# Layer 0's last steps become a stream of the written order, and the first state-space prologue moves into the two-pass steps

## The chip, the cores and the metric

The kernel runs on one NeuronCore of a Trainium2 chip. The metric is the device time in microseconds. The kernel before took 868.06 us (median of three runs, 865.57 to 869.98). The engines are called PE (matrix), DVE (vector), ACT (scalar), POOL (GpSimd) and SP (synchronisation, which here issues most transfers). Each has its own instruction queue and works it off in order.

## The reference, cut to what matters

Two batches of 256 tokens with 256 features pass two layers. All arithmetic is in 32-bit floats.

```
x = x + cross_attention(layernorm(x), ctx)       # layer 0: 16 heads of 16, 4096 context rows of 128
x = x + state_space(layernorm(x))                # conv of 4, silu, 16 states scanned over the tokens, gate, layernorm
x = x + real(ifft(fft(layernorm(x)) @ w)) + bias # spectral layer
x = x + softmax((q Wq + bq)(ctx Wk + bk)^T) (ctx Wv + bv)   # layer 1: one head, 4096 context rows
x = x + self_attention(layernorm(x))             # 16 heads, only the 5 queries with the greatest score per head are kept
x = x + mixture_of_experts(layernorm(x))         # 8 experts of 256 x 1024, 2 per token
```

The state-space layer is `h = h * A + u * b`, `y = sum over states of h * c + D * u`, for 16 states of each feature. The spectral layer is linear, so the kernel forms one 256 x 256 matrix from the transform and the weights and multiplies by it.

## The kernel before, in words

**Layer 0.** The 16 heads are taken in 4 groups of 4 heads, for 2 batches: 8 groups, `G`. Each group has 16 steps in each of two passes. The first pass computes scores with the queries in rows and only takes their maxima (`mp`, DVE). The second pass, 17 steps later, computes them with the keys in rows, with the negated maxima folded into the queries (`lowered`), exponentiates them (`exps`, ACT), multiplies by the values (`weigh`, into `av`) and adds the result up on DVE. So steps 0 to 16 do the first pass alone, steps 17 to 127 do both (the two-pass steps), and steps 128 to 145 do the second pass alone: these are the last steps. `finished` divides a group by its sums and writes its part of `O[b]`. The PSUM banks are two double tiles (`ps2`) and four single ones (`ps1`, `bank`). Small work such as new keys and values is hung onto step numbers in the table `made` and is issued at the end of its step.

**State-space layer.** `state_prologue(b)` adds layer 0's output (`add_rows`), normalises, transposes (`turned`), computes the gate, the convolution of four taps and the two silus, and the projections `bcT`. For batch 0 it avoids ACT's other function tables: the root is taken by Newton steps on DVE (`rstd_by_vector`), and silu is an exponential, an addition, a reciprocal and a product. For batch 0 it runs in the last steps, one piece for each of steps 128 to 145 (`ahead`, lines 1079 to 1081). `state_loop(b)` takes 16 states one after another: `weighted` scales by b (ACT), `into` transposes (PE), `scan` scans (DVE), `outof` transposes back and scales by c, one row tile on DVE and one on ACT, and `summed` adds ACT's one up in PSUM by a product with the identity. `state_epilogue`, `spectral_layer`, `context_scores`, `context_sums`, `self_attention` and `router` follow for each batch.

**The written order.** After the last steps, two generators hold the two batches' chains: `a` is batch 1 from its prologue on, `b` is batch 0 from its state loop on. A third, `m`, forms the spectral matrix. The string `ORDER` (line 32) says letter by letter which generator runs to its next `yield`; `in_order` makes every engine keep the order in which instructions are then issued. Each batch has four PSUM banks of its own there, and `m` shares those of batch 0. Batch 1's chain can start only when the last steps have finished `O[1]`, and its states use the room that held layer 0's `exps`.

**Shared rooms.** SBUF is reused by tag: the states of batch 0 lie where values were (`V0`), the spectral inputs where keys were (`K0`), the rows of the context (`nat`) where queries (`Q`) and then the spectral inputs were. The router's result starts the experts: twelve blocks of 128 tokens always, with weights loaded into rooms that the attention gave up.

The file records nearly every instruction through one helper, so most profile rows say L164; they are told apart by their tiles.

Of the kernel before, what the change touches and what calls it, by code (L numbers as in the profile page):

```python
# [12 lines left out]
ALU = mybir.AluOpType  # L13
# [15 lines left out]
LOWEST = -3.0e38  # L29

# [3 lines left out]
        "mbbbabbambamaabmbaabmaabaaababmbbabmababaaabaamambbbbbbaabaaaaaaaaaaaaaaaaaaabaa",  # L34
        "bbaabbabbababababbabaaaaababbbbaaaaababababbaaabbabaaabaabbabbaaaaaaaaaabbbbbbba",
        "abaabbbbbbabbabaabbabbbaabaaaaaaabababaabababaabbabbbbbbabbabbbbbaaababbbbaababb",
        "bbbababaabbabaababaababababbaabababbababaaaaabbabbaaababbbabaaabababbbaabbb",
# [5 lines left out]
def perceiver(ctx: ExitStack, tc: tile.TileContext, d: dict, out: bass.AP):  # L43
# [128 lines left out]
    def rstd_of(mv):  # L172

        n = mv.shape[1]
        r = small.tile([P, n], F32, tag="rstd", name="rstd")
        ve.tensor_scalar_add(r, mv[:, :, 1], EPS)
        ve.reciprocal(r, r)
        se.activation(r, r, AF.Sqrt)
        yield 1.0
        return r  # L180

    def rstd_by_vector(mv):
# [8 lines left out]
        yield 0.5  # L191
# [4 lines left out]
        yield 2.4  # L196
        return r

    def normalised(src, dst, rstd_of=rstd_of):
# [7 lines left out]
        yield 1.2  # L207
# [5 lines left out]
        yield 0.8  # L213

    def turned(src, dst, ps):

        for c in range(2):
            for t in range(2):
                te.transpose(
                    ps[:, c * NQ + t * P : c * NQ + (t + 1) * P], src[:, t, c * P : (c + 1) * P], ident  # L220
                )
        se.copy(dst.rearrange("p c n -> p (c n)"), ps)

# [25 lines left out]
    def lower(q, negm, ps):  # L249

        for qt in range(2):
            te.transpose(
                ps[:, qt * P : (qt + 1) * P], negm[:, qt, :, :].rearrange("p j r -> p (j r)"), ident
            )
        ve.tensor_tensor(q, q, ps[:, :NQ], ALU.add)

    def add_rows(b, src, w, bank):

        srcT = XNT(b)
        turned(src, srcT, bank("ps_tr"))  # L260
        yield 1.2
# [3 lines left out]
        yield 1.6  # L265
        ve.tensor_tensor(of(b), of(b), ps.rearrange("p (t e) -> p t e", t=2), ALU.add)
        yield 0.8
# [43 lines left out]
    def spectral_matrix(bank):  # L311


        def product(terms, dst, scale):

            ps = bank("ps_f")
            for i in range(2):
# [6 lines left out]
                yield 1.8  # L324
            se.mul(dst.rearrange("p i n -> p (i n)"), ps, scale)
            yield 0.6

        se.mul(sp["ncos"], sp["cos"], -1.0)
        yield from product([(sp["wr"], sp["cos"]), (sp["wi"], sp["sin"])], sp["reT"], 1.0)
        yield from product([(sp["wr"], sp["sin"]), (sp["wi"], sp["ncos"])], sp["nimT"], 1.0)  # L330
        yield from product([(sp["reT"], sp["cos"]), (sp["nimT"], sp["sin"])], spectral, 1.0 / D)

    def state_prologue(b, bank):
# [5 lines left out]
        turned(xn, xnT, bank("ps_tr"))  # L339
        yield 1.2  # L340
        yield 0.0
# [14 lines left out]
        for i in range(2):  # L356
            project(pg[:, i * NQ : (i + 1) * NQ], gate_w, slice(i * P, (i + 1) * P), xnT)

        for c in range(2):
            se.mul(u[:, c, :], xnT[:, c, :], cols[:, c, CONV_W + 3 : CONV_W + 4])  # L360
        yield 1.0
        for c in range(2):
# [5 lines left out]
            yield 1.3  # L368
        if b == 0:
# [5 lines left out]
            for i, (col, z, o) in enumerate(  # L375
# [4 lines left out]
                yield 1.0  # L380
                ve.tensor_scalar_add(e, e, 1.0)
                ve.reciprocal(e, e)
                for c in range(2):
                    ve.scalar_tensor_tensor(o[:, c, :], z[:, c, :], cols[:, c, col : col + 1], e[:, c, :], ALU.add, ALU.mult)
                yield 2.0
        else:
            for c in range(2):
                se.activation(u[:, c, :], u[:, c, :], AF.Silu, bias=cols[:, c, CONV_B : CONV_B + 1])
            for i in range(2):
# [3 lines left out]
            yield 1.6  # L393

        ps = bank("ps_ut")
        for t in range(2):
            for c in range(2):
                te.transpose(ps[:, t * D + c * P : t * D + (c + 1) * P], u[:, c, t * P : (t + 1) * P], ident)
        pb = bank("ps_bct")
        for t in range(2):  # L400
            project_rows(pb[:, t * 2 * NS : (t + 1) * 2 * NS], u, t, bcw)
        yield 1.2
        se.copy(ut.rearrange("p t e -> p (t e)"), ps)
        ve.tensor_tensor(
# [3 lines left out]
        yield 1.0  # L408
        U[b] = dict(u=u, ut=ut, yT=yT, ub=ub, h=h, gT=gT, hc=hc, bcT=bcT, xn=xn)

    def state_loop(b, bank, by_vector):
# [28 lines left out]
        def outof(n):  # L440

            ps = bank("ps_ht")
            for t in range(2):
                for c in range(2):
                    te.transpose(
                        ps[:, t * D + c * P : t * D + (c + 1) * P], a["h"][n % 3][:, c, t * P : (t + 1) * P], ident
                    )
            for t in range(2):
# [12 lines left out]
        weighted(0)  # L461
        into(0)
        weighted(1)
        yield 1.0
        for n in range(NS):
            scan(n)
            if n + 1 < NS:
                into(n + 1)
            if n + 2 < NS:
                weighted(n + 2)  # L470
            yield 0.9
            if n >= 1:
                outof(n - 1)
            if n >= 2:
                summed(n - 2)
            yield 0.9
        outof(NS - 1)
        summed(NS - 2)
        yield 1.0
        summed(NS - 1)  # L480
        if by_vector < 2:
            se.copy(yT[:, 1, :], yps[:, :D])
        yield 0.8

    def state_epilogue(b, bank):
        a = U[b]
        ve.tensor_tensor(of(b), of(b), rows[:, LN_B, :].unsqueeze(1).to_broadcast([P, 2, D]), ALU.add)
        y = a["ub"][0]
# [6 lines left out]
        yield 0.8  # L495
        for c in range(2):
# [3 lines left out]
            )  # L500
        ve.tensor_mul(y, y, a["gT"])
        yield 1.7

# [3 lines left out]
        zs = [ps[:, t * D : (t + 1) * D] for t in range(2)]  # L507
        for t in range(2):
            te.matmul(zs[t], lhsT=ident, rhs=a["xn"][:, t, :], start=True, stop=False)
            te.matmul(zs[t], lhsT=ident, rhs=rows[:, OUT_B, :], start=False, stop=False)  # L510
            for c in range(2):
                te.matmul(
                    zs[t], lhsT=y[:, c, t * P : (t + 1) * P], rhs=out_w[:, c, :], start=False, stop=(c == 1)
                )
        yield 2.0
        for t in range(2):
            ve.bn_stats(st[:, t, :], zs[t])
            ve.bn_aggr(mv[:, t, :], st[:, t, :])
        yield 1.3
# [9 lines left out]
        yield 1.8  # L529


    def spectral_layer(b, bank):
# [3 lines left out]
        turned(xn, xnT, bank("ps_tr"))  # L536
        yield 1.2
        ps = bank("ps_s")
        for t in range(2):
            o = ps[:, t * D : (t + 1) * D]  # L540
            te.matmul(o, lhsT=ident, rhs=rows[:, FFN_B, :], start=True, stop=False)
            for c in range(2):
                te.matmul(
                    o, lhsT=xnT[:, c, t * P : (t + 1) * P], rhs=spectral[:, c, :], start=False, stop=(c == 1)
                )
        yield 1.4
        ve.tensor_tensor(of(b), of(b), ps.rearrange("p (t e) -> p t e", t=2), ALU.add)
        yield 0.8
# [8 lines left out]
    def context_scores(b, bank):  # L557
# [3 lines left out]
        turned(xn, xnT, bank("ps_tr"))  # L561
        yield 1.2
        qT = acts.tile([P, 2, NQ], F32, tag=f"O{b}", name="qT")
        ps = bank("ps_q1")
        for i in range(2):
# [1005 lines left out]
```

## Time and profile before

| what | value |
|---|---|
| median of three runs | 868.06 us (865.57 to 869.98) |
| the profiled execution | 865.26 us |
| its span | 863.5 us |
| mean granted clock of PE | 0.973 |
| busy PE, PEld, DVE, ACT | 814.6, 586.5, 571.9, 458.8 us |
| last two-pass step ends | about 445.1 us |
| the last steps, to their last `av` addition | 445.1 to 497.7 us |
| experts begin | about 749.5 us |

PE's records include the latency of a product and overlap; its busy share therefore says less than that of DVE or ACT. [...]

### The profile page before, as it was taken

How to read it: one execution, taken by the hardware profiler on the slowest of the kernel's cores; microseconds unless marked ns; L12 is line 12 of the kernel's file. 1: busy time of each engine (PE TensorE's matmuls, PEld its weight loads, DVE VectorE, ACT ScalarE, POOL GpSimd, SP SyncE). 2: the span in 40 equal slices, each digit the busy share in tenths (PEclk: the TensorE clock that was granted, in tenths of full speed). 3: DMA queues.
4: the chain of work that ended last, by engine and by line, in shares of the span. 5: the costliest groups of instructions: out<-in, count | busy, mean ns of one | idle time of the engine just before them, and what ended most of it. 6: DMA issues, size and time to landing. Idle time of an engine off the chain costs nothing.

```text
span 863.5 us, 20999 instructions
## 1 busy us (share of the span) xinstructions
PE 814.6 (94%) x8640; PEld 586.5 (68%) x8640; DVE 571.9 (66%) x1044; ACT 458.8 (53%) x858; POOL 46.1 (5%) x108
## 2 busy tenths in 40 slices
PE   5999999999999999999999899878999999699996
PEld 3665666666666666666665478756488866499995
DVE  4788888878787878788863668985743376641112
ACT  6436666766666666666668758621642225411120
POOL 5004020000000000000000000000000000030003
PEclk9999999999999999999999989998999969889999
DMA  7216131011010010000010203000222500529602
GB/s 269 55 32 184 24 115 42 21 23 23 17 23 20 19 23 19 22 19 2 2 51 2 80 19 86 13 1 1 97 98 98 195 1 2 195 70 329 229 20 81
DMA packets 35314, 56.67 MB, mean 66 GB/s; under 512 B 5872, under 2 KB 22816, under 8 KB 35216
## 3 DMA queue, kind: packets, MB, share of 16 engines
q1 hardware_dynamic: 27904, 41.44, 15.8%
q0 software_dynamic: 3264, 10.05, 3.6%
q10 hardware_dynamic: 4048, 3.80, 1.5%
q8 instruction: 70, 1.15, 0.6%
q14 instruction: 28, 0.23, 0.1%
HBM read 42.16 MB, written 4.85 MB: 54 GB/s over the span
## 4 chain that ended last, share of the span: by engine, by line
PE 83%; DVE 8%; ACT 4%; issue 2%; DMA 1%; POOL 1%; ACTq 0%; POOLq 0%; DVEq 0%
PE ps L164 29%; PE av L164 17%; PE ps_h L1362 5%; PE ps_y L1378 4%; PE ps_s L164 4%; DVE states L164 4%; PE ps_k L164 4%; PE ps_v L164 3%; PE ps_aqk L164 2%; PE ps_am L164 2%; PE ps_pt L164 1%; PE ps_ht L164 1%; PE asc L164 1%; PE ps_q L164 1%; PE ps_f L164 1%
## 5 line engine op out<-in xcount | busy, mean ns | idle before, releaser
L164 DVE TENSOR_REDUCE mp<-ps 128x2 f32<-128x1024 f32 (+1 forms) x273 | 302.6, 1153 | 88.4 <-PE ps L164 88.4
L164 ACT ACTIVATE exps<-ps 128x512 f32<-128x512 f32 (+1 forms) x495 | 263.8, 617 | 111.4 <-PE ps L164 111.1
L164 PE MATMUL ps<-qk,KB 32*128 32x256 f32 x2048 | 250.0, 392 | 1.7 <-DVE qk L164 1.7
L164 PE MATMUL ps<-KB,qk 32*128 32x256 f32 x2048 | 244.8, 390 | 0.0
L164 PEld LDWEIGHTS ps<-KB,qk 32*128 32x128 f32 x2048 | 172.1, 184 | 52.6 <-issue 37.7
L164 PEld LDWEIGHTS ps<-qk,KB 32*128 32x128 f32 x2048 | 183.9, 184 | 13.2 <-issue 4.8
L164 PE MATMUL av<-exps,V 128*32 128x256 f32 x2048 | 137.9, 387 | 2.7 <-DVE more L164 1.6
L164 PEld LDWEIGHTS av<-exps,V 128*32 128x32 f32 x2048 | 53.9, 109 | 66.4 <-ACT exps L164 37.9
L164 DVE TENSOR_TENSOR av<-av 128x256 f32<-128x256 f32 x120 | 49.4, 412 | 20.4 <-PE av L164 20.4
L1369 ACT ACTIVATE room<-ps_h 128x512 f32<-128x512 f32 x24 | 14.2, 597 | 72.5 <-PE ps_h L1362 60.3
L1362 PEld LDWEIGHTS ps_h<-room,w 128*128 128x128 f32 x384 | 44.5, 192 | 0.5
L1362 PE MATMUL ps_h<-room,w 128*128 128x128 f32 x384 | 44.8, 275 | 0.0
L164 DVE TENSOR_TENSOR_SCAN states<-decay,ps_in 128x256 f32<-128x256 f32 x64 | 39.7, 667 | 5.4 <-PE ps_in L164 5.4
L1378 PE MATMUL ps_y<-w,room 128*128 128x256 f32 x192 | 43.3, 379 | 0.0
L164 PEld LDWEIGHTS ps_v<-l_wv,ctxT 128*128 128x128 f32 x256 | 32.6, 191 | 15.4 <-issue 6.3
L1378 PEld LDWEIGHTS ps_y<-w,room 128*128 128x128 f32 x192 | 35.6, 190 | 4.4
L164 PE MATMUL ps_v<-l_wv,ctxT 128*128 128x128 f32 x256 | 35.0, 280 | 1.2 <-ACT V L164 1.2
L164 PE MATMUL ps_k<-ctxT,wkc 128*128 128x512 f32 x64 | 35.5, 640 | 0.0
L164 PE MATMUL av<-more,nat 128*128 128x256 f32 x128 | 32.9, 381 | 0.3 <-ACT more L164 0.3
L164 ACT COPY qk<-ps_k 128x512 f32<-128x512 f32 x32 | 18.6, 587 | 25.5 <-PE ps_k L164 25.5
L164 ACT ACTIVATE states<-states,more 128x256 f32<-128x256 f32 x64 | 28.2, 498 | 6.6 <-PE ps_in L164 5.9
L164 ACT ACTIVATE aexps<-asc 128x512 f32<-128x512 f32 x32 | 17.0, 604 | 24.7 <-PE asc L164 24.7
(302 smaller groups left out, 901.1 us busy)
## 6 DMA issues: line engine op xcount, KB each, us to landing
w<-in_moe_w SPq DMA_DIRECT2D x24, 1024.0 KB, 7.7
KB<-qk SPq DMA_DIRECT2D x220, 32.0 KB, 2.0
ctxT<-in_ctxT SPq DMA_DIRECT2D x4, 512.0 KB, 8.0
ctxT<-in_ctxT POOLq DMA_DIRECT2D x4, 512.0 KB, 6.3
x_slots<-O POOLq DMA_DIRECT2D x15, 128.0 KB, 6.4
y_slots<-room ACTq DMA_DIRECT2D x10, 128.0 KB, 3.5
room<-x_slots ACTq DMA_DIRECT2D x9, 128.0 KB, 5.0
KB<-qk ACTq DMA_DIRECT2D x32, 32.0 KB, 2.0
```

Source lines behind the costliest of these rows:

```text
L164: i = getattr(self.engine, name)(*args, **kw)
L1362: nc.tensor.matmul(ps[fc // 4][:, (fc % 4) * P : (fc % 4 + 1) * P], lhsT=weights[k][0][:, c, fc * P : (fc + 1) * P], rhs=xT[k][:, c, :], s ...
L1369: nc.scalar.activation(hT[k][:, 4 * i : 4 * i + 4, :].rearrange("p f n -> p (f n)"), ps[i], AF.Silu)
L1378: nc.tensor.matmul(ps[:, :D], lhsT=hT[k][:, fc, :], rhs=weights[k][1][:, fc, :], start=(fc == 0), stop=(fc == NF - 1),)
```

## The change

1. **The last steps become a stream.** A step of layer 0 is now a generator, `attend(n)`. Steps 0 to 127 are run to their end as before. Steps 128 to 145 form a fourth stream `t`, and the written order interleaves it with `b` and `m`. In these steps the exps come in four single banks, where there were two single ones and a double one.
2. **One ring of eight banks.** All streams take their PSUM banks from one pool of eight; the four for each batch are gone.
3. **Finer steps.** Almost every instruction group has a `yield` of its own, so the written order has 879 letters where it had 315. In self-attention the exponentials and maxima now come ahead of the lowering of the next group.
4. **The first prologue** runs in steps 95 to 125: one item in each of steps 95 to 111, then two items a step from 114 to 122, one in 123 and 124, three in 125. Its gate product is copied to SBUF at once, and its reciprocals come in halves of 256 columns.
5. **Fewer products.** Batch 0's state loop takes both row tiles on DVE (`by_vector` 2), so its sums in PSUM are gone. Biases and the residual are added on DVE where identity products did it. The two projections of layer 1's queries and keys are multiplied into one small matrix beforehand (`context_maps`), so that `context_scores` needs one product from `xnT` and no `qT`.
6. The load of batch 0's context rows comes after its spectral layer, where it came after its state loop.

```diff
-        ahead = state_prologue(0, bank)
-        for n in range(NM, NM + LAG + 1):
-            made.setdefault(n, []).append((next, ahead, None))
+    AHEAD = [NM - 16 - NORM + i for i in range(NORM)] + [
+        NM - 14 + i for i, k in enumerate((2, 2, 2, 2, 2, 2, 2, 2, 2, 1, 1, 3)) for _ in range(k)
+    ]
+    ahead = state_prologue(0, lambda name: bank(name))
+    for n in AHEAD:
+        made.setdefault(n, []).append((next, ahead, None))
...
-                four = [(2, False), (0, True)]
+            four = [(2, False), (0, n < NM)]
...
-        for n in range(NM + LAG + 1):
+    for n in range(NM):
+        for _ in attend(n):
+            pass
...
-    post = ctx.enter_context(tc.tile_pool(name="post", bufs=4, space=bass.MemoryType.PSUM))
-    side = [lambda name, b=b: post.tile([P, 512], F32, tag=f"s{b}", name=name) for b in range(B)]
+    post = ctx.enter_context(tc.tile_pool(name="post", bufs=8, space=bass.MemoryType.PSUM))
+    def bank(name):
+        return post.tile([P, 512], F32, tag="s", name=name)
+    def last_steps():
+        for n in range(NM, NM + LAG + 1):
+            yield from attend(n)
+        yield from finished(behind.pop("closing"))
...
-            state_loop(0, side[0], 1), later((context_rows, 0)), state_epilogue(0, side[0]),
+            state_loop(0, bank, 2), state_epilogue(0, bank), spectral_layer(0, bank),
+            later((context_rows, 0)), context_scores(0, bank), context_sums(0, bank),
...
+        "t": last_steps,
...
+        if b == 0:
+            se.copy(gT.rearrange("p c n -> p (c n)"), pg)
+            pg = gT.rearrange("p c n -> p (c n)")
...
-                ve.tensor_scalar_add(e, e, 1.0)
-                ve.reciprocal(e, e)
+                for c in range(2):
+                    ve.tensor_scalar_add(e[:, c, :], e[:, c, :], 1.0)
+                    ve.reciprocal(e[:, c, :], e[:, c, :])
...
-            te.matmul(zs[t], lhsT=ident, rhs=a["xn"][:, t, :], start=True, stop=False)
-            te.matmul(zs[t], lhsT=ident, rhs=rows[:, OUT_B, :], start=False, stop=False)
+            project_rows(ps[:, t * D : (t + 1) * D], y, t, out_w)
+            ve.tensor_tensor(zs[t], zs[t], ps[:, t * D : (t + 1) * D], ALU.add)
...
-            project(ps[:, i * NQ : (i + 1) * NQ], x1_wq, slice(i * P, (i + 1) * P), xnT)
+            te.matmul(ps[:, :NQ], lhsT=qk_w[:, c, :], rhs=xnT[:, c, :], start=(c == 0), stop=(c == 1))
```

The new function that `m` calls first:

```
def context_maps(bank):
    ps = bank("ps_wqT")
    for e in range(2):
        for c in range(2):
            te.transpose(
                ps[:, e * D + c * P : e * D + (c + 1) * P], x1_wq[:, c, e * P : (e + 1) * P], ident
            )
    yield
    se.copy(x1_wq.rearrange("p e d -> p (e d)"), ps)
    yield
    ps = bank("ps_maps")
    col = lambda e, c: cols[:, e, c : c + 1]
    for i in range(2):
        for e in range(2):
            te.matmul(
                ps[:, i * CD : (i + 1) * CD], lhsT=x1_wq[:, e, i * P : (i + 1) * P], rhs=x1_wkT[:, e, :],
                start=(e == 0), stop=(e == 1),
            )
        yield
    lhs = [lambda e: x1_wkT[:, e, :]] + [lambda e, i=i: x1_wq[:, e, i * P : (i + 1) * P] for i in range(2)]
    lhs.append(lambda e: col(e, X1_BQ).to_broadcast([P, P]))
    for k, of_e in enumerate(lhs):
        for e in range(2):
            te.matmul(
                ps[:, 2 * CD + k : 2 * CD + k + 1], lhsT=of_e(e), rhs=col(e, X1_BK if k else X1_BQ),
                start=(e == 0), stop=(e == 1),
            )
        yield
    se.copy(qk_w.rearrange("p c n -> p (c n)"), ps[:, : 2 * CD])
    se.copy(qk_b, ps[:, 2 * CD : 2 * CD + 4])
    yield
```

## The prediction

> **What bounds the kernel now.** First the page's first two parts, for shares over time; then busy time by stretch, cut where a stage begins in the order of instructions; then the groups of instructions, for the duration of one; then the list of waits.
>
> ```profile
> PE 814.6 (94%) x8640; PEld 586.5 (68%) x8640; DVE 571.9 (66%) x1044; ACT 458.8 (53%) x858; POOL 46.1 (5%) x108
> ```
>
> PE 94% is no headroom to divide by: a matmul's record is latency, not pitch. Where nothing is late (640 to 652 us) four transposes start 0.43 us ahead of what follows, two 256-column products 0.87. So I cost PE by pitch: transpose 0.108, product of 128, 256, 512 columns 0.223, 0.433, 0.86 us, one of eight quadrant-packed products 0.128.
>
> ```profile
> 397.40:445.10 47.70, 47.66 (x754) 31.91 (x755) 42.56 (x50) 32.48 (x64) 0.00 (x0) 1.00 0.01 2
> 445.10:497.00 51.90, 47.01 (x604) 27.44 (x600) 25.75 (x63) 40.30 (x68) 0.00 (x0) 0.96 0.20 57
> 497.00:525.00 28.00, 26.20 (x151) 22.19 (x147) 18.60 (x42) 17.78 (x40) 0.00 (x0) 0.90 0.04 10
> 525.00:569.00 44.00, 39.69 (x267) 32.51 (x266) 41.52 (x78) 29.83 (x72) 0.00 (x0) 1.00 0.17 49
> 569.00:592.00 23.00, 16.65 (x65) 12.80 (x64) 15.25 (x50) 4.43 (x10) 0.00 (x0) 0.85 0.00 0
> 592.00:671.00 79.00, 78.75 (x376) 57.40 (x376) 42.67 (x124) 33.03 (x57) 1.35 (x6) 1.00 0.24 80
> 671.00:749.50 78.50, 72.18 (x561) 52.48 (x559) 50.99 (x148) 30.47 (x55) 0.00 (x0) 0.91 0.31 105
> 749.50:863.50 114.00, 101.40 (x677) 95.25 (x677) 27.91 (x103) 18.91 (x33) 15.53 (x16) 0.93 0.43 140
> ```
>
> Columns: stretch, length, busy PE, PEld, DVE, ACT, POOL, granted clock, DMA share, GB/s. Row by row: the last 16 two-pass steps (2.98 us each; PE the bound, DVE idle 47.70 - 42.56 = 5.1 us, 0.32 a step); the one-pass last steps with the first prologue; the second prologue beside the first state loop; both loops (DVE 94%); epilogues and spectral layers, where no engine passes 73%; layer 1's context attention (PE); self-attention and router; the experts. From 445.1 to 749.5 are 304.4 us.
>
> ```profile
> L164 ACT ACTIVATE exps<-ps 128x512 f32<-128x512 f32 x42 | 22.6, 598 | 8.2 <-PE ps L164 7.9
> L164 DVE RECIPROCAL states<-states 128x512 f32<-128x512 f32 x2 | 6.7, 3352 | 0.1
> L164 DVE TENSOR_TENSOR_SCAN states<-decay,ps_in 128x256 f32<-128x256 f32 x64 | 39.7, 667 | 5.4 <-PE ps_in L164 5.4
> L164 ACT ACTIVATE states<-states,more 128x256 f32<-128x256 f32 x62 | 27.4, 498 | 5.9 <-PE ps_in L164 5.9
> DVE arest L164 <- PE ps_negm L164: 7.4, 7, 1.8
> ```
>
> The mean durations are the prices below; the last row, from the waits of 671 to 749.5 us, is DVE standing at the lowering of self-attention.
>
> **The change: the first prologue moves into the two-pass steps.** Seventeen items go one to a step into steps 95 to 111, 23 more into steps 114 to 125. Each stands in DVE's queue between one step's `av` addition and the next step's maxima. DVE's maxima free the two double banks of the scores, and PE waits for those.
> Steps 95 to 111: DVE gets an addition (0.68), statistics 1.2, the root by vector 2.4, two scalings 0.74: 5.0 us, against 11.2 us of DVE idle in the 16 steps 345 to 397.4 us; hidden. PE gets 8 transposes and 4 products: 2.6 us, on the path.
> Steps 116 to 122: six convolution products (2.9 us), four additions and four reciprocals of 256 columns, four products of 0.48, two tiny ones. A reciprocal of 512 columns is 3.35 us and one of 2 columns 0.17, so 256 columns are about 1.76. Splitting pays the fixed part again: by these rows 0.16 us for each of two extra reciprocals and two extra additions, 0.64 us. [...] In all 13.0 us of DVE work in seven steps that leave 7 x 0.32 = 2.2: +10.8 us on the path[...].
> Steps 114, 115, 123 to 125: the gate product, `ps_ut` and `ps_bct`: 3.1 us of PE, on the path.
> Banks: the prologue's tiles come from the ring of four single banks. `ps_tr` twice, `ps_wo` two steps, `ps_g`, `ps_ut` two, `ps_bct` together eat eight bank-steps. With three banks left, the second half's scores wait for an exp of the first half: in the step that begins at 439.1 us PE needs the bank 1.0 us into it, and the first exp ends 1.8 us into it. Between 0 (DVE already late) and 0.9 us each, 0 to 7 us; I take 4.5, nearer the upper end because none of the eight falls in the steps where DVE is late anyway.
> Sum: the last two-pass step ends 2.6 + 10.8 + 3.1 + 4.5 = **21 us later**, at 466 us (bounds 13.5 to 26).
>
> **The last 17 steps beside batch 0's state loop.** Exps: 68 of 512 columns at 0.598 = 40.7 (pairs of 1024 at 1.034 go: +0.16 x 17 = 2.8, included), 32 weightings at 0.498 = 15.9, copies 1.2: ACT 57.5 us. PE: 272 packed products 34.8, 128 transposes 13.8, context maps and the rest 6.5: 55. DVE: 32 scans 21.3, 32 weighted sums at 0.48 = 15.4 (all by vector now, so 16 ACT scalings and 16 PE sums of 0.433 go), 17 additions 7.1, rest 4: 48. ACT decides; DVE held 94% in the loops of before, so 57.5/0.92: **63 us** (58 to 74; 74 is the 78% that ACT had in the last steps of before). What waits: each `av` addition stands ahead of scans on DVE, and each `ps_in` behind scores on PE. The 2 MB `nat` load of batch 0 now stands on SP behind nothing but the spectral loads, and comes after the spectral layer; two score passes (27 us or more) cover it. Without that cover it costs the some 10 us it took at 194 GB/s.
>
> **The second prologue and first epilogue.** Batch 1 can start only when the last steps are over. Its chain: last division 0.6, transposes and copy 1.8 (the `ncos` scaling is ahead on ACT), product with the spectral one between 2.6, addition and statistics 2.0, root with table load 1.9, scaling 0.75, transposes and copy 1.3, multiplication 1.0, convolution 2.9, table load and silu 2.3, transposes 0.7, gate silu and copies 2.2, table load and weighting 2.5, `ps_in` 0.6, hand-overs 2: **25 us** (20 to 30). Batch 0's epilogue and the spectral matrix lie beside it. Full-clock PE work is only 17.6 us here. The row: 498 to 502 us, granted clock 0.50 at 3.2 of 4 us busy; the like stretch 569 to 592 had 0.85 in the mean, which costs 17.6 x 0.15 = 2.6 us. [...] I keep the row, within the hand-overs, as most of the loss is off the chain.
>
> **Batch 1's state loop with batch 0's spectral layer and scores.** DVE: 32 scans 21.3, 16 sums 7.6, 16 score copies at 0.676 = 10.8, norms and additions 6.6: 46.3; at the 94% of before **49 us**. PE has 40, ACT 32.
>
> **Both context sums and batch 1's scores.** PE: 32 x (4 x 0.108 + 2 x 0.433) = 41.6, 16 scores 13.8, epilogue, spectral and key maps 4.6: 60; before held PE full in such a stage: **62 us** (60 to 68).
>
> **Self-attention and router.** PE 57 and DVE 43 us in both kernels. The maxima now come ahead of the lowering, so part of the 7.4 us wait goes: 2.5 of it, **76 us** (70 to 80).
>
> **Fewer products.** 16 PE sums 6.9, bias and residual products of the epilogues 3.5, of the spectral layers 1.7, query products 3.5, less 3.3 for the context maps: 12 us of PE, already in the sums. They pay only where PE binds. The three DVE bias additions for each batch (0.68) are in the DVE sums.
>
> **Sum.** 63 + 25 + 49 + 62 + 76 = 275 against 304.4: -29.4; with the 21 us, **-8.4 us**. The 114 us of experts and the 865.26 - 863.5 = 1.8 us around the span stay: 856.9 for the profiled execution. That execution is 0.3% under the median of the runs, 868.06, from which 859.7 follows; I take 858.
>
> **Rivals.**
> A. The moved prologue is mostly absorbed and the one ring lets the staggered streams pack. For it: DVE is idle 5 us in those 16 steps, and PE work from 445 on falls by about 20 us. Against: 13 us in seven steps. First pass +13.5, the rest 265: 865.3 - 26 = 839 at its far end; with half of the difference to the forecast, 848.
> B. It only shifts work: first pass +25, later stages at 279: nothing gained, 865.
> C. Slower: ACT paces the shared stage. An `av` addition waits for products that wait for exps, with scans queued behind it on DVE. At 70% ACT the stage takes 82 us, +19: 877. It decides (over 0.5% slower) once the stage passes 63 + 12.7 = 76 us. For it: ACT had only 78% in the last steps before; against: a stream with scans to run fills DVE now, and all eight banks are open to every stream.
> D. The stagger does nothing since both streams still end together: that is B's sum.
>
> **How the numbers follow.** About 0.5% is what a measurement here can tell from no change. Forecast (-14 to -4.3 us) 0.42, A 0.24, B and D 0.16, C 0.18: faster 0.66, same 0.16, slower 0.18. Range 841 to 873, leaving out the ends of A and C; the forecast's own is 852 to 864.
>
> **What would show it.** Right: steps 116 to 122 at some 4.5 us with DVE full; last two-pass step near 466; batch 0's loop over at about 529; first scan of batch 1 near 554, its last near 603; router near 741; the expert stretch 114 us. Wrong: two-pass steps still at 3 us (A), the shared stage at 76 us or more (C), or an expert stretch that grows because weights come late.

## The result, and the profile after

The changed kernel takes 853.03 us (median of four runs, 852.59 to 855.07) beside 867.9 us for the kernel before: a ratio of 0.9834, with a 95% interval of 0.9804 to 0.9864. That is 14.4 us less by the measured ratio. The forecast was 858 us, and 8.4 us less for the profiled execution. The profiled execution is the longest of the four, 855.07 us with a span of 853.3 us; before it was 865.26 and 863.5. So the profiles differ by 10.2 us, and the sums below are made against those.

From the page of the changed kernel, busy time of each engine:

```profile
PE 801.2 (94%) x8596; PEld 572.7 (67%) x8596; DVE 581.5 (68%) x1072; ACT 451.8 (53%) x858; POOL 46.3 (5%) x108
```

Shares are as before, and say nothing of where the time went. Busy time by stretch does (columns as in the prediction: stretch, length, busy PE, PEld, DVE, ACT, POOL, granted clock of PE (1.00 is full rate), DMA share, GB/s), cut where the same stages begin:

```profile
409.10:472.90 63.80, 57.54 (x774) 36.55 (x774) 54.48 (x71) 37.00 (x74) 0.00 (x0) 1.00 0.01 2
472.90:531.00 58.10, 56.69 (x721) 38.14 (x717) 39.24 (x85) 48.94 (x105) 0.00 (x0) 1.00 0.08 25
531.00:594.50 63.50, 57.57 (x315) 44.20 (x312) 54.61 (x138) 33.96 (x72) 0.00 (x0) 1.00 0.22 62
594.50:665.80 71.30, 66.30 (x339) 50.03 (x338) 43.80 (x121) 31.93 (x56) 0.67 (x3) 1.00 0.27 89
665.80:738.20 72.40, 67.10 (x571) 49.55 (x569) 50.16 (x148) 28.50 (x53) 0.69 (x3) 0.94 0.34 117
738.20:853.30 115.10, 100.21 (x672) 94.06 (x672) 27.83 (x103) 18.07 (x32) 15.96 (x16) 0.93 0.41 137
```

The first row holds the same 16 two-pass steps as the first row shown of before: 63.8 us instead of 47.7, with DVE idle for 9.3 us in spite of its added work. In the second row last steps and batch 0's loop lie together, and ACT is busy for 84% of it, where no row shown of before has more than 78%. The third row is the second prologue and batch 1's loop (first scan at 551.6 us), the fourth both context sums, the fifth self-attention and router, the last the experts.

From the groups of 409.1 to 531 us, by shape, the reciprocals, and from the waits of 665.8 to 738.2 us the one that was shown of before:

```profile
L172 DVE RECIPROCAL states<-states 128x256 f32<-128x256 f32 x4 | 7.0, 1753 | 0.1
```

```profile
DVE arest L172 <- PE ps_negm L172: 2.1, 2, 1.7
```

A reciprocal of 256 columns costs 1.753 us (1.76 was interpolated), and the wait at self-attention's lowering fell from 7.4 us to 2.1.

Times of single two-pass steps are read below from the `av` additions on DVE, one in each step from 19 on except the first of a group, which copies instead: what a step hangs onto DVE's queue stands between its addition and the next. In the last of these steps the additions come 3 us apart in the kernel before.

### The profile page after: what moved, and what is told of

Read it like the earlier page. It is cut to its first block, busy times and chain, and to the rows that moved or that the text cites. A ratio compares the mean times of both kernels' runs of the same rounds, so it can differ in the third digit from the quotient of the medians.

```text
span 853.3 us, 20944 instructions
## 1 busy us (share of the span) xinstructions
PE 801.2 (94%) x8596; PEld 572.7 (67%) x8596; DVE 581.5 (68%) x1072; ACT 451.8 (53%) x858; POOL 46.3 (5%) x108
## 4 chain that ended last, share of the span: by engine, by line
PE 82%; DVE 10%; ACT 4%; issue 2%; DMA 1%; POOL 1%; POOLq 0%; ACTq 0%; DVEq 0%
PE ps L172 29%; PE av L172 17%; PE ps_h L1466 5%; PE ps_y L1482 4%; PE ps_k L172 4%; PE ps_v L172 3%; PE ps_s L172 3%; DVE mp L172 3%; DVE states L172 2%; PE ps_aqk L172 2%; PE ps_in L172 2%; PE ps_pt L172 1%; PE ps_f L172 1%; PE ps_ht L172 1%; PE asc L172 1%
## 5 line engine op out<-in xcount | busy, mean ns | idle before, releaser
L172 ACT ACTIVATE exps<-ps 128x512 f32<-128x512 f32 x512 | 266.6, 602 | 131.0 <-PE ps L172 130.7
L172 PE MATMUL ps<-qk,KB 32*128 32x256 f32 x2048 | 260.7, 397 | 3.4 <-ACT exps L172 1.7
L172 PE MATMUL ps<-KB,qk 32*128 32x256 f32 x2048 | 251.4, 395 | 4.5 <-DVE mp L172 4.5
L172 PEld LDWEIGHTS ps<-qk,KB 32*128 32x128 f32 x2048 | 187.8, 186 | 18.1 <-ACT exps L172 5.2
L172 PE MATMUL ps_s<-ctxT,xn 128*128 128x512 f32 x64 | 29.5, 594 | 0.0
L172 ACT COPY V<-ps_v 128x512 f32<-128x512 f32 x32 | 18.8, 587 | 20.1 <-PE ps_v L172 15.1
```

The lines of the kernel that those rows point to most:

```text
L172: i = getattr(self.engine, name)(*args, **kw)
```

## The experiments

Each is the changed kernel with one edit. The kernel before was measured beside each, and its median moved between 867.6 and 870.4 us, so ratios to it compare better than times.

**What the reciprocals cost in their place.** `e9_tanh` replaces them by ACT's Tanh:

```diff
-AF.Exp, bias=minus[:, 1 - i, c : c + 1], scale=-1.0)
+AF.Tanh, bias=minus[:, 1 - i, c : c + 1], scale=0.5)      # minus now holds half of the bias
-ve.tensor_scalar_add(e[:, c, :], e[:, c, :], 1.0)
-ve.reciprocal(e[:, c, :], e[:, c, :])
+ve.tensor_scalar(e[:, c, :], e[:, c, :], 1.0, 0.5, ALU.add, ALU.mult)
```

> The four reciprocals of the first prologue go, and nothing else moves: the sigmoid comes from ScalarE's Tanh, which needs no other table than the exps (half of 1 + tanh of half the argument; the addition of 256 columns becomes an addition and a multiplication in one instruction). This measures the reciprocals in their place. Theory of the prediction (VectorE over-full by 10.8 us in steps 116 to 122, of which 4 x 1.75 = 7.0 are reciprocals): the four long steps (5.3, 5.3, 4.5, 5.3 us in the changed kernel) fall to 3.3 to 3.7, first pass 6.5 to 7 us shorter, 846 to 847. Rival (those steps are as long by ps_g's and the exps' hand-overs, and e1_silu gained by spreading the convolution): steps above 4.3 us, time 850 or more.

Measured: 848.48 us, ratio 0.9747 (0.9715 to 0.978), against 0.9834 for the changed kernel; the difference is some 7.5 us of 868, and the intervals do not overlap. The timeline of DVE in the changed kernel (start, duration, instruction; idle time before it would stand in brackets behind it):

```profile
442.94 0.41 DVE L172 TENSOR_TENSOR av<-av 128x256 f32<-128x256 f32 x1
443.27 0.29 DVE L172 TENSOR_SCALAR states<-states 128x256 f32<-128x256 f32 x1
443.59 1.75 DVE L172 RECIPROCAL states<-states 128x256 f32<-128x256 f32 x1
445.26 0.78 DVE L172 SCALAR_TENSOR_TENSOR more<-more,cols,states 128x256 f32<-128x256 f32 x2
445.96 2.35 DVE L172 TENSOR_REDUCE mp<-ps 128x2 f32<-128x1024 f32 x2
448.23 0.41 DVE L172 TENSOR_TENSOR av<-av 128x256 f32<-128x256 f32 x1
```

and the same stretch in `e9_tanh`:

```profile
441.56 0.41 DVE L172 TENSOR_TENSOR av<-av 128x256 f32<-128x256 f32 x1
441.89 0.28 DVE L172 TENSOR_SCALAR states<-states 128x256 f32<-128x256 f32 x1
442.09 0.87 DVE L172 SCALAR_TENSOR_TENSOR more<-more,cols,states 128x256 f32<-128x256 f32 x2
442.88 2.35 DVE L172 TENSOR_REDUCE mp<-ps 128x2 f32<-128x1024 f32 x2
445.15 0.41 DVE L172 TENSOR_TENSOR av<-av 128x256 f32<-128x256 f32 x1
```

No row has idle time: DVE is full, and each instruction pushes the next maxima. From addition to addition 5.29 us become 3.59; the four steps together fall from 20.4 to 13.6 us, 6.8 for four reciprocals of 1.75; the step behind them takes 0.7 more than in the changed kernel. Tanh asked for no table load of its own: the trace of this run has 13 table loads, as that of the changed kernel has.

**The same gain by other means, and a trap.** `e1_silu` takes ACT's Silu instead, and one convolution product a step:

```diff
-(2, 2, 2, 2, 2, 2, 2, 2, 2, 1, 1, 3)
+(2, 1, 2, 1, 1, 1, 1, 1, 4, 1, 1, 2)      # pieces in steps 114 to 125; fourth from the right: the silus and ps_ut
```

> The first prologue's two sigmoids (exp on ScalarE, then additions, reciprocals and products on VectorE in steps 119 to 122) are replaced by the Silu of ScalarE that batch 1 uses, all four in step 122; the six convolution products go one to a step (116 to 121). Theory of the prediction (steps 116 to 122 are late because VectorE is over-full, 13.0 us of work in a slack of 2.2): conv leaves 6 x (0.48 - 0.32) = 1 us, ScalarE has about 0.95 us free in a step and gets two table loads of 1.28 and four silus of 0.43 = 4.3, so +3.4 in step 122; the 10.2 us that steps 116 to 123 lost in the changed kernel become 4.4, steps 116 to 121 take 3.0 to 3.2 us, and the time falls by about 6 us, to 847. Rival (banks and PE work make those steps late, not VectorE's reciprocals): steps 116 to 121 stay above 3.3 us and the time is within 2 us of 853. Rival (the table loads hold the exps and with them both halves of two steps): step 122 alone costs over 7 us, time 850 or more.

Measured: 855.49 us (849.24 to 857.05), ratio 0.9852: no gain. The profiled execution is the fastest of the five; why the other four take 6 to 8 us more, no trace shows. In it the six steps ahead of the silus fell to 2.98 us each, as the theory has it, but the step with the silus took 9.3 us and the next nearly 6. From the timeline of PE in `e1_silu`:

```profile
444.99 1.30 PE L172 MATMUL ps_ut<-ident,states 128*128 128x128 f32 x4 [2.16 <-ACT states L172]
446.81 0.63 PE L172 MATMUL ps<-KB,qk 32*128 32x256 f32 x2
447.24 0.63 PE L172 MATMUL ps<-KB,qk 32*128 32x256 f32 x2
```

The transposes `ps_ut` had come into the same step, and PE stood for 2.16 us at ACT's table load and silus, with the scores behind in its queue. The pairs of products there start 0.43 us apart where 0.21 is usual: half rate (the granted clock is 0.83 in the mean of 440 to 450 us, and 1.00 from 430 to 440). `e8_silu_later` moves `ps_ut` one step on:

```diff
-(2, 1, 2, 1, 1, 1, 1, 1, 4, 1, 1, 2)
+(2, 1, 2, 1, 1, 1, 1, 1, 3, 1, 1, 3)
```

> As e1_silu, but the transposes of u (ps_ut) come one step after the silus, not in the same step: there PE stood at ps_ut from about 443.5 to 448.3 us, for ScalarE's table load and silus. Theory: without that stand the step with the silus costs 3.4 us (4.3 of ScalarE work less 0.95 of slack), [...]the clock stays at 1.00 there; first pass 3 us shorter than in e1_silu, and the runs no longer spread by 8 us; 846 to 848. Rival (the exps behind the table loads hold the scores' banks, so PE stands as long without ps_ut): the step costs 6 us as in e1_silu, 853 to 856.

Measured: 850.94 us, ratio 0.9801, 2 to 3 us better than the changed kernel, though the intervals overlap. The step with the silus takes 6.2 us and the next 6.0, together 6 us over. From 443.1 to 447.4 us ACT has two table loads of 1.28 us and the four silus, and PE's timeline shows it standing at the exps behind them:

```profile
448.07 1.25 PE L172 MATMUL av<-exps,V 128*32 128x256 f32 x16 [3.28 <-ACT exps L172]
```

The clock, forecast to stay at 1.00, is 0.64 from 449.8 to 453.2 us. So the stand at `ps_ut` was one part of the trap, and the rival's part, exps held behind the table loads, is the other; 3.4 us was too little for it.

**Banks held over a step.** `e7_at_once`:

```diff
-[NM - 16 - NORM + i for i in range(NORM)]
+[NM - 16 - NORM + i for i in (0, 0, 2, 2, 2, 3, 4, 5, 6, 7, 8, 9, 10, 11, 14, 14, 16)]
-(2, 2, 2, 2, 2, 2, 2, 2, 2, 1, 1, 3)
+(2, 2, 2, 2, 2, 2, 2, 2, 2, 0, 5)
```

> The first prologue's pieces that share a bank go into one step each (transposes with their copy, both output products with the addition; at the end ps_ut, ps_bct and what reads them), so that no bank is held from one two-pass step into the next; the work is the same. In the changed kernel these steps are longer by 1.1, 1.6, 2.1 (output products), 1.0 (second transposes) and 2.9 us (ps_ut and ps_bct), 8.7 together, of which PE work is 0.4 + 1.7 + 0.4 + 1.3 = 3.8. Theory of the prediction (banks held over a step are 4.5 us): these steps cost about 4 us in all, first pass 4 to 5 us shorter, 848. Rival (what costs is PE's own work and the handing over behind it, wherever it stands): 8 to 9 us as before, 853. Rival (VectorE stands at an addition whose products come late, and the next maxima behind it): longer by 2 us or more.

Measured: 848.33 us, ratio 0.9771 (0.9747 to 0.9796). Steps 94 to 112, which the prologue's first half had made 6.7 us longer than before, are 3.1 longer now; steps 123 to 125 give back another 2.1. So 5.7 us was the holding of banks and what waits for it. What stays, 3.1 and 1.4 us, is near PE's own work there, 2.6 and some 1.4 by the forecast's prices.

**Half of the prologue back beside the last steps.** `e2_half`:

```diff
-AHEAD = [...17 items...] + [...23 items in steps 114 to 125...]
+AHEAD = [...17 items...]
-state_loop(0, bank, 2), state_epilogue(0, bank), ...
+ahead, state_loop(0, bank, 2), state_epilogue(0, bank), ...      # one more b behind each of the first 22 t
```

> Half of the first prologue goes back out of the two-pass steps: normalisation and transposes stay in steps 95 to 111; gate product, convolution, sigmoids, ps_ut and ps_bct become the first 22 pieces of stream b, one after each of the first 22 pieces of the last steps. Theory of the prediction: the first pass ends 10.8 + 3.1 + about 2.5 = 16 us earlier; the shared stage gets 13 us of VectorE work ahead of the first scan (first scan 12 to 15 us after the stage begins, not 3), its end is set by ScalarE work that cannot begin before, so the stage grows from 60 to about 70; net -6, 847. Rival (moving it ahead was worth its cost: the stage is a chain of scans, and every us of later start is a us of later end, plus the lost cover of the last steps): stage 76 or more, time 853 to 860. Rival (absorbed: VectorE and ScalarE catch up, stage 62): 839.

Measured: 857.19 us, ratio 0.9881 (0.9831 to 0.9931). By the `av` additions the steps from 94 on take 16.1 us less, as forecast. The shared stage of `e2_half`:

```profile
454.80:532.90 78.10, 65.33 (x741) 43.76 (x738) 51.64 (x106) 53.04 (x115) 0.00 (x0) 0.91 0.06 20
```

It is 20 us longer than the 58.1 of the changed kernel, with PE at 84% of it. No scan can start before the prologue is through: the first comes 25.0 us after the stage begins, in the changed kernel 3.9. The last steps do not fill this time in the order as written, for their `av` additions of steps 127, 128 and 129 come 14.4 and 12.2 us apart, behind the prologue's pieces in DVE's queue, and the granted clock is 0.50 from 470 to 480 us. So in this order the moved half is worth its price in the two-pass steps by some 4 us: the four runs are all slower than the four of the changed kernel, but the intervals overlap. An order that runs more last steps ahead of the prologue's pieces wasn't tried.

**Last steps first.** `e3_t_first`:

```diff
-for which in ORDER:
+for which in "t" * 126 + ORDER.replace("t", ""):
```

> Same work, same pieces, but the last steps run to their end before any piece of the other streams; the rest of the written order is kept. Theory of the prediction (the gain of the later stages is overlap: 63 us for last steps and state loop together): last steps alone 68 exps x 0.598 = 40.7 at some 90% ScalarE, 45 us; then batch 0's loop, 45 to 49 us beside batch 1's prologue, which can begin at 45 and not at 60: of the 34 us lost, some 12 come back because batch 1 starts earlier; +15 to +25, 868 to 878, slower than before the change. Rival (the gain is the fewer products and the one ring; the stagger gives nothing): within 4 us of 853.

Measured: 868.59 us, ratio 0.9998 (0.9979 to 1.0016): the whole gain is gone. Last steps alone, then batch 0's loop and batch 1's prologue:

```profile
471.00:514.00 43.00, 40.35 (x575) 22.56 (x575) 10.47 (x30) 36.81 (x73) 0.00 (x0) 1.00 0.17 51
514.00:564.20 50.20, 43.35 (x247) 34.86 (x248) 46.36 (x106) 24.71 (x54) 0.00 (x0) 0.90 0.08 21
```

DVE has next to nothing to do in the first and is full in the second, ACT the other way round. From the end of the first pass to batch 1's first scan it is 93.2 us, in the changed kernel 472.9 to 551.6 or 78.7; what follows is 2.6 us longer than there. So taking the overlap out costs 14.5 us in this order. That may be more than the overlap alone is worth: batch 1's prologue was expected to begin with the end of the last steps, but the order kept the letters of `a` behind batch 0's loop. `O[1]` is finished at 513.4 us, and PE's timeline has batch 1's output products only here:

```profile
547.92 1.89 PE L172 MATMUL ps_wo<-l_wo,xnT 128*128 128x256 f32 x8
```

An order that starts batch 1 at 514 us wasn't tried.

**Which engine paces the shared stage.** `e4_one_sum`:

```diff
-state_loop(0, bank, 2)
+state_loop(0, bank, 1)
```

> Batch 0's state loop sums half of its weighted states on ScalarE and PE again, as in the kernel before (16 scalings of 0.498 us on ScalarE and 16 products of 0.433 on PE come back, 16 VectorE sums of 0.48 go). Theory of the prediction (ScalarE paces the shared stage): +8 us on the stage, 861; the stage goes from 60 to about 67. Rival (PE's ordering paces it): +7 by PE's products, with ScalarE under 80%; told apart by the busy shares. Rival (VectorE's queue paces it, scans behind additions): 4 us or more faster, 849.

Measured: 861.85 us, ratio 0.992; the shared stage is 65.4 us:

```profile
471.70:537.10 65.40, 63.99 (x727) 42.07 (x728) 33.75 (x71) 53.50 (x117) 0.00 (x0) 1.00 0.08 24
```

The price was foretold to 1 us. Its cause isn't settled: the edit loads ACT and PE alike, ACT stays at 82% (84% in the changed kernel) and PE's records fill the stretch in both. The edit also keeps one of the eight banks, `yps`, through the whole loop, which neither theory nor rivals counted. Only the rival with DVE is out.

**One ring or two.** `e6_two_rings`:

```diff
-post = ...tile_pool(name="post", bufs=8, ...)      # one tag for all streams
+post = ...tile_pool(name="post", bufs=4, ...)      # tag s1 for a and t, tag s0 for b and m
```

> The eight banks of the later stages in two rings of four, as in the kernel before (stream a and the last steps in one, stream b and the matrix in the other), all else as changed. Theory of the prediction (all eight banks open to every stream is a part of what keeps the shared stage short): the second half's scores of a last step wait for its first exps again; shared stage 64 to 70 us in place of 60, the others up to 3 us longer each; 858 to 866. Rival (in a written order each bank is free long before its turn, the ring's shape does nothing): within 2 us of 853. Rival (one ring holds a stream up behind a bank that the other stream keeps): 850 or less.

Measured: 877.3 us, ratio 1.0095 (1.0067 to 1.0122), 24 us more than the changed kernel. The shared stage and self-attention with the router:

```profile
473.10:545.50 72.40, 65.32 (x721) 41.84 (x718) 39.40 (x85) 49.37 (x105) 0.00 (x0) 1.00 0.07 21
681.00:763.00 82.00, 73.73 (x570) 51.75 (x568) 50.92 (x148) 28.69 (x53) 0.68 (x3) 0.96 0.30 103
```

Work is equal to the changed kernel's; the stage is 14 us longer, self-attention and router 10. From the waits of the shared stage (engine and what it is about to write, what it waited for: total, times, longest):

```profile
ACT exps L172 <- PE ps L172: 20.9, 16, 3.4
DVE states L172 <- PE ps_ht L172: 19.4, 11, 2.2
DVE av L172 <- PE av L172: 11.0, 12, 2.6
```

The first two of these waits in the changed kernel, where the third is 2.6 us:

```profile
ACT exps L172 <- PE ps L172: 7.4, 10, 1.6
DVE states L172 <- PE ps_ht L172: 13.4, 11, 1.8
```

With four banks the scores wait for exps, `av` for scores, and scans stand behind `av` in DVE's queue. This order was written for one ring; an order written for two rings may lose less, and wasn't tried.

**Fewer products, the other part.** `e12_bias_products` brings the identity products of epilogues and spectral layers back:

```diff
-project_rows(ps[:, t * D : (t + 1) * D], y, t, out_w)
+te.matmul(z, lhsT=ident, rhs=a["xn"][:, t, :], start=True, stop=False)
+te.matmul(z, lhsT=ident, rhs=rows[:, OUT_B, :], start=False, stop=False)
+for c in range(2): te.matmul(z, lhsT=y[:, c, t * P : (t + 1) * P], rhs=out_w[:, c, :], start=False, stop=(c == 1))
```

> The bias and residual products of the epilogues and spectral layers come back (12 products of 256 columns, 5.2 us of PE), and the VectorE additions that took their place go (2 x 2.2 us). Theory of the prediction (fewer products pay only where PE binds, and these stand where no engine is full: batch 0's beside batch 1's prologue and loop, where VectorE paces, batch 1's in a chain of its own): batch 0's share does nothing or gains 1 us, batch 1's costs 0 to 1.5 us of PE on its chain less 1 us of VectorE; time within 2 us of 853. Rival (PE paces these stages, and the 5.2 us are on the path): 857 to 858.

Measured: 852.98 us, ratio 0.981 (0.9777 to 0.9843): no change that can be told. Counted from batch 0's first scan, batch 1's first comes 1.7 us later than in the changed kernel, its last 2.2, and the router's end 0.4: what is lost in one stage is covered in a later one.

**PE's clock.** Between before and after, 4.9 us of the difference arise at 67 to 77 us, where both kernels run the same instructions. The rows of before, after and `e5_fill`:

```profile
67.50:77.50 10.00, 10.00 (x146) 7.00 (x150) 7.82 (x8) 6.67 (x13) 7.90 (x20) 1.00 0.78 259
```

```profile
67.50:77.50 10.00, 9.62 (x66) 6.14 (x70) 3.97 (x5) 3.86 (x8) 8.64 (x24) 0.51 0.75 265
```

```profile
67.50:77.50 10.00, 10.00 (x146) 6.75 (x145) 7.93 (x9) 6.67 (x13) 7.71 (x22) 1.00 0.74 252
```

In the second, PE is busy for 9.62 of 10 us at half rate (granted clock 0.51) and gets 66 products done where 146 are done in the others at 1.00. `e5_fill` puts unread products where PE stands, and so tests whether want of work takes the clock down:

```diff
+def busy(times, lhsT, rhs):
+    ps = bank("ps_busy")
+    for _ in range(times):
+        te.matmul(ps[: lhsT.shape[-1], : rhs.shape[-1]], lhsT=lhsT, rhs=rhs, start=True, stop=True)
```

> Products that nobody reads are put where PE has nothing to do: two of 512 columns behind the first lowering of the maxima (the gap at 66.2 to 67.9 us), six of 256 columns behind the last output products of self-attention (gap 729.9 to 732.8), three of 512 behind the router's products (738.5 to 741.6), two of 512 behind the counting products (742.6 to 744.7). In the changed kernel the granted clock falls to 0.50 from 67.5 to 77.3 us and from some 732.5 to 750 us; before, from 746 to 759. Theory ([...]work at half rate costs half of its time): clock 1.00 at both places, 4.9 us less at the first, about 1 at the transposes, 1.9 at the router's products, 2 to 3 in the first expert products; time 843 to 846. Rival (the clock falls for a reason that PE's idleness does not set, such as what the other engines or the memory do): the clock falls all the same, and the time is 853 or up to 3 us more by the added products.

Measured: 850.77 us, ratio 0.9801; the profiled execution 847.83. The clock is 1.00 at the first place; at the second, ahead of the experts, it is 0.86 where it was 0.60, and the first expert products take 5.6 us instead of 8.0. The mean clock is 0.991 to 0.993 in all four runs, where the four of the changed kernel have 0.979 to 0.982. So what PE was given to do moved the clock here, and the rival is out. The first place alone would not show it, since `e7_at_once` keeps 1.00 there without such products. The gain is 2 to 3 us and not 8, and the intervals overlap. What the traces offer for the rest, none of it tested alone: half rate costs nothing where PE has nothing to do (from 738.2 to 752.6 us of the changed kernel, at a clock of 0.60, its records cover 9.28 of 14.4 us), the third product behind the router's came 0.8 us too long, and the first two experts show 1.2 us of new gaps in PE, whose cause isn't known.

**Together.** `e10_tanh_once` is `e9_tanh` with `e7_at_once`; `e11_all_three` adds `e5_fill` (two products behind the router's).

> e9_tanh and e7_at_once together. If the two costs are separate terms (VectorE's reciprocals in steps 116 to 122, banks held over steps in 95 to 111 and 123 to 125), the gains add: 853 - 6.5 - 4.7 = 842. Rival (the second hides behind the first, or the first pass meets another bound): 845 or more.

> e10_tanh_once with the unread products of e5_fill (two instead of three behind the router's products, since in e5_fill the counting products began 0.8 us late behind them). If the clock's losses are apart from the other two terms, 842 - 2.3 (what e5_fill gained in its median) = 840, and clock 1.00 at 67 to 77 us in each run. Rival (the experts' first weights come too late for an earlier start, as the gaps of 0.3 to 0.6 us in e5_fill's first expert say, so that what is gained ahead is lost there): 842 or more, with PE gaps of 2 us or more in the first two experts.

Measured: 843.67 us, ratio 0.9695 (0.9673 to 0.9718), and 837.81 us, ratio 0.9636 (0.9619 to 0.9654). In units of the earlier comparisons (867.9 us) 0.9695 is 841.4: the terms add, to within the 2 us that the interval leaves. `e11_all_three` beats both kernels, the changed one by 2.0% (0.9636/0.9834). Its clock is 1.00 at 67 to 77 us. The time is below both numbers. PE's gaps in the first two experts are 1.7 us, a little under the 2 that the rival named, and behind them the clock is 0.53 from 742.1 to 745.5 us, so that these experts take 14.6 us where the changed kernel takes 10.6. Late weights are not the reason: the last load ahead of them is issued at 704.2 us, none takes over 13.1 us to land, and the first product comes at 731.9. What else makes the gaps isn't known. Its two-pass steps:

```profile
393.10:454.00 60.90, 60.12 (x855) 39.72 (x857) 51.54 (x75) 40.41 (x80) 0.23 (x1) 1.00 0.01 2
```

The row is 17 two-pass steps, from step 109 on, of some 61 us; they took 70.9 us in the changed kernel and 53.4 before. PE stands for 0.8 us of them only.

## Why the prediction was right, and where its steps were off

| step of the sum | forecast | profiled |
|---|---|---|
| last two-pass step ends later by | 21 | 27.8, of it 4.9 the clock at 67 to 77 us |
| last steps beside batch 0's loop | 63 | 58.1 |
| second prologue, to batch 1's first scan | 25 | 20.6 |
| batch 1's loop | 49 | 42.9 |
| both context sums | 62 | 71.3 |
| self-attention and router | 76 | 72.4 |
| experts | 114 | 115.1 |

- **First pass.** Without the clock it is 22.9 us, and the parts stand nearly: steps 116 to 122 cost 9.8 us by the `av` additions (10.8 forecast for VectorE), the first half 6.7 (4.9 forecast: 2.6 of PE and half of 4.5 for banks), gate, `ps_ut` and `ps_bct` with their banks 6.4 (5.4). `e9_tanh` and `e7_at_once` took two of the terms away singly: the four steps lost 6.8 us for 7.0 of reciprocals, and banks were 5.7 us, not 4.5. The first half of rival A (absorbed) is out.
- **Shared stage.** ACT's work was counted as 57.5 us, and the stage has 48.9. The mis-sized term is the duration taken for a pitch, the time from one start to the next: on ACT one instruction's record overlaps the next one's, as these rows of ACT's timeline in the changed kernel show, and four exps take 2.04 us and not 4 x 0.598, four weightings 1.72 and not 4 x 0.498. With these 68 exps and 32 weightings are 48.4 us. At the 92% of the forecast that would make 53 us, and the stage took 58.1: that ACT decides is not shown, and which engine paces the stage stays open (`e4_one_sum`).

```profile
476.40 2.04 ACT L172 ACTIVATE exps<-ps 128x512 f32<-128x512 f32 x4
478.31 1.72 ACT L172 ACTIVATE states<-states,more 128x256 f32<-128x256 f32 x4
```

  The ground given against rival C, eight banks open to every stream, was the right one: with two rings the stage takes 72.4 us and the kernel is slower than before. The prediction named the ring as a help and gave it no number; in an order written for one ring, taking it away cost more than any other edit.
- **Second prologue.** 25 us was too much. The chain counted three table loads, and two of them run while DVE still works on what ACT waits for (1.28 us each, 2.6 of the 4.4 us). From ACT's timeline of the changed kernel:

```profile
534.79 1.28 ACT L172 ACT_TABLE_LOAD   x1
539.55 0.20 ACT L172 ACTIVATE rstd<-rstd 128x2 f32<-128x2 f32 x1 [3.48 <-DVE rstd L172]
544.78 1.28 ACT L172 ACT_TABLE_LOAD   x1 [1.14 <-DVE states L172]
```

  The clock, for which the hand-overs were to leave room, cost nothing here. PE is busy for all of 540 to 555 us, the spectral products filling it, and the granted clock is 1.00 from 531 to 594.5. Here the row of 498 to 502 us, with its 0.50, misled: it came from a stretch with one stream.
- **Batch 1's loop** was held to be bound by DVE at 94%; it has DVE at 86% and is 6 us shorter. Of the 46.3 us of DVE work that were put there, 36.8 lie in it; part of batch 0's norms and additions lies ahead of the first scan, and three of its 32 score records behind the last.
- **Both context sums** is the term that was most in error. PE was put as full from the first us. Its first 23 us are not:

```profile
594.50:617.50 23.00, 18.00 (x95) 13.74 (x94) 16.78 (x47) 12.14 (x23) 0.00 (x0) 1.00 0.28 92
```

  Batch 1's epilogue and spectral layer are a chain from engine to engine there that the other stream doesn't fill, and PE is full for the 48.3 us behind it. The sum had 60 us of PE work and 2 of idle time; the stretch has 66.3 by the records, which include latency (from 640 to 650 us four transposes are recorded as 0.60 us, and what follows them starts after 0.44), and 5.0.
- **Self-attention.** 2.5 us were taken off for the wait at the lowering; it fell by 5.3, and the stretch is 3.6 us shorter than forecast.
- **Experts.** Weights come in time: the last load ahead of the experts is issued at 722.3 us, none takes over 13.3 us to land, and the first product comes at 752.6. The 1 us is a wait of 1.92 us of PE for DVE's mask of the second shared block, since all eight transposes of masks now stand together.
- **Fewer products** do not pay in the epilogues (`e12_bias_products`), as was said of places where PE doesn't bind. In the state loop taking both row tiles on DVE pays 7 to 9 us (`e4_one_sum`), but that the products are the reason is not shown.

That the total came so near is in part luck. Overlap was under-rated by 15 us in three stages and 4 in a fourth, and context sums by 9 the other way, so that the later stages took 265.3 us, not 275: the 265 that rival A gave them. The first pass took 6.8 us more than forecast, 4.9 of it the clock at 67 to 77 us, where no instruction of the change runs; without this fall the profiles would differ by some 15 us and not by 10.2. The mechanism of the first pass holds by experiments; the gain behind it is shown as a whole (`e3_t_first`, `e6_two_rings`), and its split between overlap, ring and fewer products is not.

## What to carry to other kernels

Work moved into a full stage is paid there, by the engine that has least slack: find its idle time for one step, and spread or thin out the work until each step fits (here a reciprocal of 1.75 us against 0.3 us of slack; tanh, with the same 13 table loads, did away with it). Count PSUM banks by how long they are held, and from which ring: splitting the one ring in two cost 24 us here, more than the whole change had gained, though in an order written for one. Where a queue is in program order, whatever waits in it takes all behind it along, and on PE a wait of 2.16 us was followed by half rate besides (`e1_silu`, pairs of products 0.43 us apart and not 0.21).

## What the runs showed of the hardware

From 66 to 78 us half rate lasted 3.4, 6.8 or 10.2 us. In slices of 0.25 us the first fall begins between 66.0 and 69.25 us and lasts 3.4 us in `e2_half`, `e4_one_sum` and `e12_bias_products`, 6.8 in `e1_silu`, `e3_t_first` and `e8_silu_later`, 10.2 in the changed kernel, `e6_two_rings`, `e9_tanh` and `e10_tanh_once`; it is absent in before and in `e7_at_once`, all with the same instructions up to there. Why the same instructions fare differently from profile to profile, no run here shows. Before and the changed kernel have much the same idle time ahead of it: PE is busy for 1.16 and 1.09 of the 3.5 us from 64 to 67.5 us, and the longest gap is 1.67 us in both. And in the changed kernel the clock stayed down for 10.2 us while PE's records show no gap from 67.88 us on. Nothing here shows which measure of PE's work the clock goes by; the products of these steps use 32 rows each.
